# Transfers of the first batches in one queue, weights centred early, and another place for the queries' turn, in a cross-attention kernel in fp32

## The chip, the core and the metric

One core of a Trainium2 chip runs the kernel. The metric is the device time in microseconds of one execution, here the median of three runs. The core has five engines that run side by side, each in the order of its own instructions: TensorE (PE) for matmuls, with results in PSUM; VectorE (DVE); ScalarE (ACT); GpSimd (POOL); and SyncE (SP), which here only issues transfers. Everything is fp32.

## What is computed

For each of 64 batches there are 256 text rows x of width 512 and 256 context rows c of width 384. The reference, cut to what matters (scale is 1/sqrt(512)):

```python
text_p  = einsum('bld,dh->blh', H_l, W_text) + b_text
audio_p = einsum('bsd,dh->bsh', H_a, W_audio) + b_audio
Q = layer_norm(text_p, g1, beta1)
K = layer_norm(audio_p, g2, beta2)
V = audio_p
alpha = softmax(einsum('blh,bsh->bls', Q, K) * scale)
H_hyper = einsum('bls,bsh->blh', alpha, V)
H_hyper = einsum('blh,hk->blk', H_hyper, W_out) + b_out
return layer_norm(H_hyper + H_l, g_out, beta_out)
```

## The kernel before

**Projections.** Queries and keys are projected (`ps_q`, `ps_k`), their bias is added, and each row is normalised. The first two batches use `Projection`: whole products, with mean and variance from VectorE's statistics (`moments`, line 234). From the third on `Blocks` (line 409) is used: W_text, W_audio and their biases have had the mean of each of their rows taken away ("centred"), so that a projected row has mean zero and only its squares are summed (`square`, on ScalarE). `Blocks` computes the 2 x 2 block product with seven instead of eight block products; their left sides come from sums over the turned input (`sum_x`, `sum_c`), their right sides from sums over the weights (`weight_sums`), all on GpSimd. `products` writes one PSUM bank of the pool `p_pj` (four banks) for up to two block products; `leave(n)` (line 431) adds block product n into the rows on VectorE, and when both block products of a bank have left, the bank is free for a later `products`.

**Turning.** A matmul contracts over the partitions, so the normalised rows have to be turned. They are stored to DRAM (`store`: `qd`, `kd`), fetched back by four transfers with the rows in squares of 32 (`fetch`: `qq`, `kq`), turned by VectorE in 32 x 32 squares (`turn`: `qT`, `kT`, lines 91 and 394), and ScalarE applies gamma and beta (`affine`, line 401). The inputs of a later batch are loaded in squares (`load_squares`, eight transfers) and turned the same way (`turn_x`, `turn_c`); the exponentials too (`store_e`, `fetch_e`, `turn_e`). Batch 0 is turned by TensorE instead (`turn_rows`).

**Folding.** W_audio and W_out are multiplied once (`turn_weights`, `fold_multiply`, three parts), so that the context `ps_z` = c^T e needs one product more, `ps_y`, for the output. The bias of it is `bao` (`bias_parts`, `fold_bias`).

**Order.** Nothing is planned by a program: the order is that of the text, and each engine keeps it. A prologue treats batches 0 and 1 and the weights. Then the loop runs over b = 0 to 61. In iteration b TensorE does the scores of b, the block products of the queries of b+2, the context of b-1, the block products of the keys of b+2, and the two output products of b-1. Queries and keys of b+1 were normalised and stored an iteration before; here they are fetched, turned and given gamma and beta. The last two batches have their own code, where TensorE turns the exponentials (`transpose_e`).

**Queues.** Nearly all transfers are issued by SyncE, in order, and a transfer that waits for its data holds all behind it. The five bias and gain rows (`ba`, `bt`, `bo`, `go`, `beo`: `row`, broadcast to 128 partitions, 256 KB each) and the five `vectors` are issued by ScalarE among its own work. Eight semaphores serve all transfers in turn, in the order of the program: a transfer is issued only when the one eight places before it has landed, whichever engine issues it.

**PSUM.** Eight banks: `p_pj` four, `p_at` two (scores, context, turns by TensorE), `p_y` two (output, fold).

Of the kernel before, what the change touches and what calls it, by code (L numbers as in the profile page):

```python
# [15 lines left out]
P = 128  # L16
SQ = 32
# [5 lines left out]
def kernel(  # L23
# [72 lines left out]
    def load_squares(b):  # L96
        xq = blk.tile([P, L // SQ, D // NQ], F32, tag="xq", name=f"xq_{b}")
        cq = blk.tile([P, S // SQ, DA // NQ], F32, tag="cq", name=f"cq_{b}")
        squares(xq, x[b])
        squares(cq, c[b])  # L100
        return xq, cq
# [23 lines left out]
    def row(v, name):  # L125
        t = const.tile([P, H], F32, tag=name, name=name)
        nc.scalar.dma_start(t, v.rearrange("(o h) -> o h", o=1).broadcast_to([P, H]))
        return t
# [7 lines left out]
    nc.sync.dma_start(c_0, c[0].rearrange("(t p) d -> p t d", p=P))  # L136
    wa_sb = weight_by_square(w_audio, AC, "wa", nc.sync)
    ba_sb = row(b_audio, "ba")
    nc.sync.dma_start(x_0, x[0].rearrange("(t p) d -> p t d", p=P))
    wt_sb = weight_by_square(w_text, DC, "wt", nc.sync)  # L140
    blocks = {1: load_squares(1)}
    wo_sb = weight_by_square(w_out, HC, "wo", nc.sync)

    columns = const.tile([P, 5, HC], F32, tag="columns", name="columns")

    def load_columns():
        for n, v in enumerate((g1, beta1, g2, beta2, b_audio)):
# [19 lines left out]
    def turn_rows(rows_sb, chunks, name, copy):  # L167

        ar = work.tile([P, 2, chunks, P], F32, tag="y" if chunks == DC else "kT", name=f"{name}r")
        T = work.tile([P, chunks, 2 * P], F32, tag=name, name=f"{name}_0")  # L170
        for t in range(2):
            arrange(ar[:, t], rows_sb[:, t, :], chunks, copy)
        for lo in range(0, chunks, 2):
            n = min(2, chunks - lo)
            ps = p_at.tile([P, 2, 2 * P], F32, tag="at", name="ps_rows")
            for j in range(n):
                for t in range(2):
                    nc.tensor.transpose(ps[:, j, bass.ts(t, P)], ar[:, t, lo + j, :], ident)
            nc.scalar.copy(T[:, lo : lo + n, :], ps[:, :n, :])
        return T  # L180

# [44 lines left out]
    def fold_bias(part):  # L226

        ps = p_y.tile([P, D], F32, tag="y", name="ps_bao")
# [73 lines left out]
    class Projection:  # L302


        def __init__(self, name, b, srcT, w_sb, bias, nch, nt):
# [3 lines left out]
            self.centred = b > 1  # L309
# [144 lines left out]
    class Attention:  # L454
# [4 lines left out]
        def scores(self):  # L459
            self.sc = p_at.tile([P, LT, S], F32, tag="at", name="ps_sc")  # L460
# [43 lines left out]
        def transpose_e(self):  # L504
            self.ps_e = p_at.tile([P, ST, L], F32, tag="at", name="ps_e")
# [79 lines left out]
    def text(b, xT):  # L585
        return Projection("q", b, xT, wt_sb, bt_sb, DC, LT)

    def audio(b, cT):
        return Projection("k", b, cT, wa_sb, ba_sb, AC, ST)

# [269 lines left out]
```

## Time and profile before

| what | us |
|---|---|
| median of 3 runs (lowest, highest) | 1468.34 (1467.51, 1476.27) |
| the profiled execution: time, span | 1472.76, 1471.0 |
| first matmul | 8.58 |
| first scores | 53.33 |
| second scores | 72.85 |
| third scores | 100.64 |
| scores of the last iteration's successor (batch 62) | 1427.40 |
| last scores (batch 63) | 1443.66 |
| mean granted TensorE clock | 0.995 |

The profile is one execution. Each matmul in fp32 appears as several records (x16 for eight score products). "Releaser" is what ended an engine's idle time. PEld is the load of the stationary operand, which goes on beside matmuls.

### The profile page before, as it was taken

To read this page: it belongs to the slowest core of one execution; us is meant where nothing else is said; L and a number is where in the kernel's file an instruction comes from. 1 tells how busy PE (TensorE), PEld (TensorE's weight loads), DVE (VectorE), ACT (ScalarE), POOL (GpSimd) and SP (SyncE) were. 2 spreads that over 40 slices of the span, in tenths; PEclk is the share of its full clock that TensorE was granted. 3 is DMA by queue.
4 is the path that set the end of the run, shared out by engine and by line. 5 is a ranking of instruction groups with operands and counts; after the bars stand their busy time and mean duration, and the time that the engine had idled before them with its cause. 6 is when DMAs were issued, how large, how long until landed. Compare 5 with 4: busy or idle time off the path is not lost. (4 is left out here: it accounts for less than half of the span.)

```text
span 1471.0 us, 20463 instructions
## 1 busy us (share of the span) xinstructions
PE 1437.6 (98%) x5777; PEld 1097.4 (75%) x5777; DVE 1213.2 (82%) x2077; ACT 697.1 (47%) x1663; POOL 692.6 (47%) x1037
## 2 busy tenths in 40 slices
PE   7999999999999999999999999999999999999996
PEld 3577877877877777877877777777777777877873
DVE  4768888888888788888888797888888888888886
ACT  2435445445455355455455354355455355355352
POOL 1544454454454454454454453554554554454452
PEclk9999999999999999999999999999999999999999
DMA  8587777777787788887887777877877877878872
GB/s 193 151 223 204 225 233 213 230 234 205 242 241 201 236 236 207 240 233 208 237 243 199 238 231 201 242 209 226 245 223 211 246 232 214 239 216 224 241 217 80
DMA packets 450260, 322.41 MB, mean 219 GB/s; under 512 B 154724, under 2 KB 382564, under 8 KB 450148
## 3 DMA queue, kind: packets, MB, share of 16 engines
q1 hardware_dynamic: 449328, 319.79, 76.7%
q10 hardware_dynamic: 820, 1.32, 0.5%
q8 instruction: 47, 0.77, 0.2%
q14 instruction: 65, 0.53, 0.1%
HBM read 204.09 MB, written 116.92 MB: 218 GB/s over the span
## 5 line engine op out<-in xcount | busy, mean ns | idle before, releaser
L297 POOL TENSOR_SCALAR ve<-var 128x2 f32<-128x2 f32 x124 | 26.9, 217 | 680.3 <-ACT junk L335 680.3
L542 PE MATMUL ps_y<-wao,zT 128*128 128x512 f32 x768 | 340.3, 592 | 0.0
L401 ACT ACTIVATE qT<-qT,columns 128x256 f32<-128x256 f32 x256 | 132.9, 589 | 404.7 <-DVE qT L91 404.7
L542 PEld LDWEIGHTS ps_y<-wao,zT 128*128 128x128 f32 x768 | 145.8, 190 | 156.1 <-issue 142.8
L463 PEld LDWEIGHTS ps_sc<-kT,qT 128*128 128x128 f32 x1024 | 195.2, 191 | 55.1 <-issue 22.7
L463 PE MATMUL ps_sc<-kT,qT 128*128 128x256 f32 x1024 | 232.4, 380 | 1.5 <-ACT zT L532 1.5
L438 DVE TENSOR_TENSOR kr<-ps_k,kr 128x512 f32<-128x512 f32 x372 | 185.3, 512 | 24.7 <-DVE kr L438 0.9
L91 DVE STREAM_TRANSPOSE qT<-qq 128x1024 f32<-128x1024 f32 x64 | 79.7, 1245 | 151.0 <-DMA qq<-qd 151.0
L438 DVE TENSOR_TENSOR qr<-ps_q,qr 128x512 f32<-128x512 f32 x372 | 182.4, 504 | 14.7 <-PE ps_q L427 3.8
L525 PE MATMUL ps_z<-eT,c 128*128 128x256 f32 x768 | 176.6, 379 | 0.8 <-ACT eT L514 0.7
L480 ACT ACTIVATE e<-ps_sc,nmx 128x256 f32<-128x256 f32 x128 | 59.5, 469 | 238.0 <-DVE nmx L473 238.0
L427 PE MATMUL ps_q<-wtsum,xsum 128*128 128x256 f32 x744 | 170.7, 379 | 0.0
L427 PE MATMUL ps_k<-wa,cT 128*128 128x256 f32 x620 | 164.6, 380 | 0.0
L604 POOL TENSOR_TENSOR x<-x,bao 128x512 f32<-128x512 f32 x128 | 161.0, 1280 | 3.5 <-DMA x<-in_x_dram 3.5
L525 PEld LDWEIGHTS ps_z<-eT,c 128*128 128x128 f32 x768 | 145.8, 190 | 21.6 <-ACT eT L514 0.9
L427 PEld LDWEIGHTS ps_q<-wtsum,xsum 128*128 128x128 f32 x744 | 141.4, 190 | 19.2
L299 POOL TENSOR_TENSOR rstd<-ve,nhalf 128x2 f32<-128x2 f32 (+1 forms) x193 | 136.6, 708 | 16.0
L401 ACT ACTIVATE kT<-kT,columns 128x256 f32<-128x256 f32 x256 | 132.2, 591 | 3.4 <-DVE kT L91 3.4
L427 PEld LDWEIGHTS ps_k<-wa,cT 128*128 128x128 f32 x620 | 118.2, 191 | 16.2
L427 PE MATMUL ps_q<-wt,xT 128*128 128x256 f32 x496 | 117.2, 379 | 0.0
L363 ACT ACTIVATE kr<-kr,rstd 128x512 f32<-128x512 f32 x124 | 82.8, 715 | 69.9 <-POOL rstd L299 69.9
L427 PE MATMUL ps_k<-wasum,csum 128*128 128x256 f32 x372 | 102.6, 385 | 11.0 <-DVE qr L438 11.0
(113 smaller groups left out, 2228.6 us busy)
## 6 DMA issues: line engine op xcount, KB each, us to landing
x<-in_x_dram SPq DMA_DIRECT2D x64, 512.0 KB, 4.9
kd<-kr SPq DMA_DIRECT2D x64, 512.0 KB, 7.0
kq<-kd SPq DMA_DIRECT2D x256, 128.0 KB, 3.0
qd<-qr SPq DMA_DIRECT2D x64, 512.0 KB, 7.2
qq<-qd SPq DMA_DIRECT2D x256, 128.0 KB, 2.6
xq<-in_x_dram SPq DMA_DIRECT2D x252, 128.0 KB, 2.8
out_dram<-y SPq DMA_DIRECT2D x63, 512.0 KB, 6.0
c<-in_ctx_dram SPq DMA_DIRECT2D x64, 384.0 KB, 5.4
```

The source lines that it names most:

```text
L91: nc.vector.transpose(dst.rearrange("p k (b j) -> p b k j", j=SQ), src.rearrange("p b (k i) -> p b k i", k=chunks),)
L297: nc.gpsimd.tensor_scalar(ve, var, EPS, None, ALU.add)
L299: nc.gpsimd.tensor_tensor(r, ve, nhalf[:, :n], ALU.pow)
L363: nc.scalar.mul(row, row, self.r[t])
L401: nc.scalar.activation(self.T[:, k, :], self.T[:, k, :], AF.Identity, bias=bet[:, k : k + 1], scale=gam[:, k : k + 1],)
L427: nc.tensor.matmul(bank[:, j, :], lhsT=side, rhs=w, start=(i == 0), stop=(i == len(pairs) - 1))
L438: add = lambda o, i0, i1: nc.vector.tensor_tensor(o, i0, i1, ALU.add)
L463: nc.tensor.matmul(self.sc[:, t, :], lhsT=self.qT[:, k, bass.ts(t, P)], rhs=self.kT[:, k, :], start=(k == 0), stop=(k == HC - 1),)
L480: nc.scalar.activation(self.e[:, t, :], self.sc[:, t, :], AF.Exp, bias=self.nmx[:, t : t + 1], accum_out=self.den[:, t : t + 1],)
L525: nc.tensor.matmul(ps[:, j, :], lhsT=self.c_sb[:, s, bass.ts(lo + j, P)], rhs=self.eT[:, s, :], start=(s == 0), stop=(s == ST - 1),)
L542: nc.tensor.matmul(ps, lhsT=self.zT[:, k, bass.ts(t, P)], rhs=wao_sb[:, k, :], start=(k == 0), stop=(k == AC - 1),)
L604: nc.gpsimd.tensor_tensor(xb[:, t, :], xb[:, t, :], bao_sb, ALU.add)
```

## The change

- `row` and the five `vectors` are issued by SyncE. c of batch 0 is loaded in two halves, with W_audio between them. The other transfers of the prologue stand in the order in which their data is wanted; W_out and `bo` go behind the store of the keys of batch 0, and `go`, `beo` to the end of the prologue. `load_squares` takes c before x.
- `RowTurn` takes the place of `turn_rows`: batch 0 is turned row tile by row tile, each followed by its product.
- `means` is done on ScalarE (a sum with scale -1/512), and `centre` adds. W_audio and `ba` are centred, and the weight sums made, before the keys of batch 1; W_text and `bt` before its queries. Batch 1 is then projected by `Blocks`.
- Two parts of the fold stand before the queries of batch 1, the third behind them.
- In the loop the fetches of queries and keys of b+1 are issued behind `store_e` instead of ahead of the scores. `q[b + 1].turn()` stands behind all seven `leave` and `square` of the queries of b+2 (it stood between `leave(5)` and `leave(3)`), and its `affine` behind the context's copies.
- At the end, the last scores and both `transpose_e` take banks of `p_pj`, and `fold_bias` does too.

The diff, cut; the functions `text` and `audio` are gone, and `at`, `done`, `last` are the batches b, b-2 and b-1:

```diff
     def load_squares(b):
         xq = blk.tile([P, L // SQ, D // NQ], F32, tag="xq", name=f"xq_{b}")
         cq = blk.tile([P, S // SQ, DA // NQ], F32, tag="cq", name=f"cq_{b}")
+        squares(cq, c[b])
         squares(xq, x[b])
-        squares(cq, c[b])
         return xq, cq
 ...
-        nc.scalar.dma_start(t, v.rearrange("(o h) -> o h", o=1).broadcast_to([P, H]))
+        nc.sync.dma_start(t, v.rearrange("(o h) -> o h", o=1).broadcast_to([P, H]))
 ...
     c_0 = cin.tile([P, ST, DA], F32, tag="c", name="c_0")
-    nc.sync.dma_start(c_0, c[0].rearrange("(t p) d -> p t d", p=P))
+    c_rows = c[0].rearrange("(t p) d -> p t d", p=P)
+    nc.sync.dma_start(c_0[:, :1], c_rows[:, :1])
     wa_sb = weight_by_square(w_audio, AC, "wa", nc.sync)
+    nc.sync.dma_start(c_0[:, 1:], c_rows[:, 1:])
     ba_sb = row(b_audio, "ba")
     nc.sync.dma_start(x_0, x[0].rearrange("(t p) d -> p t d", p=P))
     wt_sb = weight_by_square(w_text, DC, "wt", nc.sync)
+    bt_sb = row(b_text, "bt")
     blocks = {1: load_squares(1)}
-    wo_sb = weight_by_square(w_out, HC, "wo", nc.sync)
-
     columns = const.tile([P, 5, HC], F32, tag="columns", name="columns")
-
-    def load_columns():
-        for n, v in enumerate((g1, beta1, g2, beta2, b_audio)):
-            nc.scalar.dma_start(
-                vectors[n * HC : (n + 1) * HC].rearrange("k (q i) -> k q i", q=NQ),
-                v.rearrange("(q k i) -> k q i", q=NQ, i=SQ),
-            )
+    for n, v in enumerate((g1, beta1, g2, beta2, b_audio)):
+        nc.sync.dma_start(
+            vectors[n * HC : (n + 1) * HC].rearrange("k (q i) -> k q i", q=NQ),
+            v.rearrange("(q k i) -> k q i", q=NQ, i=SQ),
+        )
 ...
+    class RowTurn:
+
+
+        def __init__(self, rows_sb, chunks, name):
+            self.rows, self.chunks = rows_sb, chunks
+            tag = "y" if chunks == DC else "kT"
+            self.ar = work.tile([P, 2, chunks, P], F32, tag=tag, name=f"{name}r")
+            self.T = work.tile([P, chunks, 2 * P], F32, tag=name, name=f"{name}_0")
+
+        def tile(self, t):
+            ar = self.ar[:, t]
+            arrange(ar, self.rows[:, t, :], self.chunks, nc.vector.tensor_copy)
+            ps = p_at.tile([P, self.chunks, P], F32, tag="at", name="ps_rows")
+            for j in range(self.chunks):
+                nc.tensor.transpose(ps[:, j, :], ar[:, j, :], ident)
+            nc.scalar.copy(self.T[:, :, bass.ts(t, P)], ps)
 ...
-        mv = const.tile([P, n, 2], F32, tag=name, name=name)
+        m = const.tile([P, n], F32, tag=name, name=name)
         for k in range(n):
-            moments(mv, rows[:, k, :], k)
-        return mv
-
-    def centre(rows, mv, n):
+            junk = work.tile([P, H], F32, tag="junk", name="junk")
+            nc.scalar.activation(
+                junk, rows[:, k, :], AF.Identity, scale=-1.0 / H, accum_out=m[:, k : k + 1]
+            )
+        return m
+
+    def centre(rows, m, n):
         for k in range(n):
-            nc.vector.tensor_scalar(rows[:, k, :], rows[:, k, :], mv[:, k, 0:1], None, ALU.subtract)
+            nc.vector.tensor_scalar(rows[:, k, :], rows[:, k, :], m[:, k : k + 1], None, ALU.add)
 ...
-            self.centred = b > 1
+            self.centred = b > 0
 ...
-    cT[0] = turn_rows(c_0, AC, "cT", nc.vector.tensor_copy)
-    bt_sb = row(b_text, "bt")
-    load_columns()
-    k[0] = audio(0, cT.pop(0))
+    c_turn = RowTurn(c_0, AC, "cT")
+    x_turn = RowTurn(x_0, DC, "xT")
+    k[0] = Projection("k", 0, c_turn.T, wa_sb, ba_sb, AC, ST)
+    q[0] = Projection("q", 0, x_turn.T, wt_sb, bt_sb, DC, LT)
+    c_turn.tile(0)
     k[0].multiply(0)
-    xT[0] = turn_rows(x_0, DC, "xT", nc.vector.tensor_copy)
+    c_turn.tile(1)
+    k[0].multiply(1)
+    mean_wa = means(wa_sb, AC, "mwa")
+    k[0].evict(0)
     war = blk.tile([P, AC, HC, P], F32, tag="kq", name="war")
     for a in range(AC):
         arrange(war[:, a], wa_sb[:, a, :], HC, nc.gpsimd.tensor_copy)
-    mean_wa = means(wa_sb, AC, "mwa")
-    k[0].evict(0)
-    k[0].multiply(1)
+    x_turn.tile(0)
+    x_turn.tile(1)
     k[0].evict(1)
     k[0].scales()
-    q[0] = text(0, xT.pop(0))
     q[0].multiply(0)
-    k[0].normalise()
-    k[0].store()
-    cT[1] = turn_c(1)
-    q[0].evict(0)
     q[0].multiply(1)
-    xT[1] = turn_x(1)
-    q[0].evict(1)
-    q[0].scales()
-    k[0].fetch()
-    g1_sb, be1_sb, g2_sb, be2_sb, bac_sb = take_columns()
-
-    for v in (g2_sb, be2_sb):
-        nc.vector.tensor_scalar(v, v, scale, None, ALU.mult)
-    waT = turn_weights()
-    q[0].normalise()
-    q[0].store()
-    mean_wt = means(wt_sb, DC, "mwt")
-    k[1] = audio(1, cT.pop(1))
-    for t in range(ST):
-        k[1].multiply(t)
-        k[1].evict(t)
-    k[1].scales()
-    bo_sb = row(b_out, "bo")
-    k[1].normalise()
-    q[0].fetch()
-    k[1].store()
-    blocks[2] = load_squares(2)
-    k[1].fetch()
-    k[0].turn()
-    k[0].affine(g2_sb, be2_sb)
-    q[1] = text(1, xT.pop(1))
-    q[1].multiply(0)
-    q[1].evict(0)
-    q[1].multiply(1)
-    part = bias_parts()
-    q[1].evict(1)
-    q[1].scales()
-    q[0].turn()
-    centre(wt_sb, mean_wt, DC)
-    fold_multiply(0)
-    fold_multiply(1)
-    fold_evict(0)
-    q[1].normalise()
-    q[1].store()
-    q[1].fetch()
-    q[0].affine(g1_sb, be1_sb)
-    fold_evict(1)
-    fold_multiply(2)
-    fold_evict(2)
-    wt_blocks = weight_sums(wt_sb, DC // 2, "wtsum")
-    xT[2] = turn_x(2)
-    xs = {2: sum_x(xT[2])}
-    for v, name in ((bt_sb, "mbt"), (ba_sb, "mba")):
-        v = v.rearrange("p (o h) -> p o h", o=1)
-        centre(v, means(v, 1, name), 1)
-    blocks[3] = load_squares(3)
-    bao_sb = fold_bias(part)
+    ba_row = ba_sb.rearrange("p (o h) -> p o h", o=1)
+    bt_row = bt_sb.rearrange("p (o h) -> p o h", o=1)
+    mean_ba = means(ba_row, 1, "mba")
     centre(wa_sb, mean_wa, AC)
     wa_blocks = weight_sums(wa_sb, 1, "wasum")
     for n, k2 in ((2, 0), (3, 1), (5, 1), (4, 0)):
         wa_blocks[n].append(wa_sb[:, 2, k2 * H2 : (k2 + 1) * H2])
+    k[0].normalise()
+    k[0].store()
+    wo_sb = weight_by_square(w_out, HC, "wo", nc.sync)
+    bo_sb = row(b_out, "bo")
+    k[0].fetch()
+    blocks[2] = load_squares(2)
+    mean_wt = means(wt_sb, DC, "mwt")
+    mean_bt = means(bt_row, 1, "mbt")
+    centre(ba_row, mean_ba, 1)
+    q[0].evict(0)
+    cT[1] = turn_c(1)
+    cs = {1: sum_c(cT[1])}
+    q[0].evict(1)
+    q[0].scales()
+    centre(wt_sb, mean_wt, DC)
+    centre(bt_row, mean_bt, 1)
+    waT = turn_weights()
+    wt_blocks = weight_sums(wt_sb, DC // 2, "wtsum")
+    q[0].normalise()
+    q[0].store()
+    q[0].fetch()
+    xT[1] = turn_x(1)
+    xs = {1: sum_x(xT[1])}
+    k[1] = Blocks("k", 1, cs.pop(1), wa_blocks, ba_sb)
+    k[1].products(1, 2)
+    k[1].leave(1)
+    k[1].products(6, 5)
+    k[1].leave(6)
+    k[1].leave(2)
+    k[1].leave(5)
+    k[1].products(7, 3)
+    k[1].leave(3)
+    k[1].leave(7)
+    k[1].products(4)
+    g1_sb, be1_sb, g2_sb, be2_sb, bac_sb = take_columns()
+    k[1].leave(4)
+    k[1].square()
+    k[1].scales()
+
+    for v in (g2_sb, be2_sb):
+        nc.vector.tensor_scalar(v, v, scale, None, ALU.mult)
+    k[0].turn()
+    k[1].normalise()
+    k[1].store()
+    k[1].fetch()
+    k[0].affine(g2_sb, be2_sb)
+    blocks[3] = load_squares(3)
+    fold_multiply(0)
+    fold_evict(0)
+    fold_multiply(1)
+    fold_evict(1)
+    part = bias_parts()
+    xT[2] = turn_x(2)
+    xs[2] = sum_x(xT[2])
     cT[2] = turn_c(2)
-    cs = {2: sum_c(cT[2])}
+    cs[2] = sum_c(cT[2])
+    q[0].turn()
+    q[0].affine(g1_sb, be1_sb)
+    q[1] = Blocks("q", 1, xs.pop(1), wt_blocks, bt_sb)
+    q[1].products(1, 2)
+    q[1].leave(1)
+    q[1].products(6, 5)
+    q[1].leave(6)
+    q[1].leave(2)
+    q[1].leave(5)
+    q[1].products(7, 3)
+    q[1].leave(3)
+    q[1].leave(7)
+    q[1].products(4)
+    q[1].leave(4)
+    q[1].square()
+    q[1].scales()
+    fold_multiply(2)
+    fold_evict(2)
+    bao_sb = fold_bias(part)
+    q[1].normalise()
+    q[1].store()
+    q[1].fetch()
     go_sb = row(g_out, "go")
     beo_sb = row(beta_out, "beo")
 ...
         at = Attention(b)
-        if b:
-            q[b + 1].fetch()
-            k[b + 1].fetch()
         at.scores()
 ...
         at.exponentials()
         at.store_e()
+        if b:
+            q[b + 1].fetch()
+            k[b + 1].fetch()
         at.fetch_e()
 ...
         q2.products(7, 3)
-        q[b + 1].turn()
-        q[b + 1].affine(g1_sb, be1_sb)
-        q2.products(4)
         q2.leave(3)
         q2.leave(7)
+        q2.products(4)
         q2.leave(4)
+        q2.square()
+        q[b + 1].turn()
         at.reciprocals()
         if last:
             last.context()
-        q2.square()
+        q[b + 1].affine(g1_sb, be1_sb)
 ...
-        ps = p_y.tile([P, D], F32, tag="y", name="ps_bao")
+        ps = p_pj.tile([P, D], F32, tag="pj", name="ps_bao")
 ...
-            self.ps_e = p_at.tile([P, ST, L], F32, tag="at", name="ps_e")
+            self.ps_e = p_pj.tile([P, ST, L], F32, tag="pj", name="ps_e")
 ...
-    end.scores()
+    end.scores(end=True)
```

More of the change, by code (lines that the diff above doesn't have):

```diff
@@ L165, in arrange @@
         )
[L167 to L180, printed above, removed]
+    class RowTurn:
[11 more added lines that the diff above has]
+            nc.scalar.copy(self.T[:, :, bass.ts(t, P)], ps)
     def turn_weights():
@@ L457, in __init__, with scores @@
             self.xb, self.c_sb = rows[b]
-        def scores(self):
-            self.sc = p_at.tile([P, LT, S], F32, tag="at", name="ps_sc")
+        def scores(self, end=False):
+            if end:
+                self.sc = p_pj.tile([P, LT, S], F32, tag="pj", name="ps_sc")
+            else:
+                self.sc = p_at.tile([P, LT, S], F32, tag="at", name="ps_sc")
             for t in range(LT):
@@ L583, in store @@
             )
[L585 to L589, printed above, removed]
     def turn_x(b):
```

## The prediction

> **What bounds the kernel now.** I read the page first, then TensorE's waits, then TensorE's rows in order of time, then the rows of all engines around its longest wait, then one undisturbed iteration, and last the end of the run. The page's totals say that TensorE is the bound:
>
> ```profile
> span 1471.0 us, 20463 instructions
> PE 1437.6 (98%) x5777; PEld 1097.4 (75%) x5777; DVE 1213.2 (82%) x2077; ACT 697.1 (47%) x1663; POOL 692.6 (47%) x1037
> ```
>
> So only 33.4 us are idle, and a change can take away idle time, time at a lowered clock, or matmul work, and little else. The chain of waits gives the work of one iteration of the loop, at full clock:
>
> ```profile
> 1013.30 6.04 PE ps_q L427 x28
> 1021.94 4.75 PE ps_k L427 x22
> 1026.69 5.15 PE ps_y L542 x12
> 1031.84 3.45 PE ps_sc L463 x16
> ```
>
> The context product lies between the first two (8.64 - 6.04 = 2.60), so an iteration is 21.99, and 1009.85 to 1031.84 in the chain is just that: nothing but matmuls. Of the 62 loop iterations, the first has no context and no output product (14.24), the other 61 have 21.99. TensorE's waits:
>
> ```profile
> PE ps_k L427 <- DVE qr L438: 11.0, 11, 3.1
> PE ps_rows L178 <- DVE cTr L162: 8.6, 1, 8.6
> PE ps_sc L463 <- ACT zT L532: 1.5, 1, 1.5
> PE ps_k L317 <- DMA wa<-in_L_xattn_W_audio_dram: 1.3, 1, 1.3
> PE ps_q L317 <- DMA wt<-in_L_xattn_W_text_dram: 0.9, 1, 0.9
> ```
>
> The first row is the one in the loop. Score products start at 53.33, 72.85 and 100.64 in TensorE's rows, and at 1427.40 behind the loop. So the first iteration took 19.52 (5.28 over its work), the second 27.79 (5.80 over), and the other 60 took 1326.76, 7.4 over 60 x 21.99. The first two, in the rows in order of time:
>
> ```profile
> 52.67 0.35 ACTq L127 DMA_DIRECT2D go<-in_L_xattn_g_out_dram  x1
> 56.48 1.33 SPq L88 DMA_DIRECT2D kq<-kd  x3
> 57.91 0.40 SPq L373 DMA_DIRECT2D qd<-qr  x1
> 61.54 1.78 SPq L88 DMA_DIRECT2D qq<-qd  x4
> 66.03 1.25 DVE L91 STREAM_TRANSPOSE qT<-qq 128x1024 f32<-128x1024 f32 x1 [4.11 <-DMA qq<-qd]
> 67.19 1.64 DVE L438 TENSOR_TENSOR qr<-ps_q,qr 128x256 f32<-128x256 f32 x3
> 68.45 1.19 PE L427 MATMUL ps_k<-wasum,csum 128*128 128x256 f32 x2 [2.88 <-DVE qr L438]
> 72.85 4.42 PE L463 MATMUL ps_sc<-kT,qT 128*128 128x256 f32 x16
> ```
>
> VectorE sits in the turn of the queries (line 91) until their fetch lands; three block sums stand behind it (`leave` 3, 7, 4), and these free the PSUM banks for which the audio products wait. The fetch is late because SyncE stood 9.7 us in a wait for `go`, which ScalarE issued only at 52.67 (SyncE's own waits). After each such wait the granted clock is lower (0.76 and 0.55 in 65 to 75 us, 0.66 in 90 to 95). In a late iteration the same turn waits too, mostly without reaching TensorE:
>
> ```profile
> 1021.75 1.25 DVE L91 STREAM_TRANSPOSE qT<-qq 128x1024 f32<-128x1024 f32 x1 [2.37 <-DMA qq<-qd]
> ```
>
> **The change, part by part.** Times from the span's start.
>
> *The start (c split, `ba` behind it in the same queue).* The first audio product began at 11.62, with 384 KB of c, 768 KB of W_audio and 256 KB of `ba` before or beside it. Now 192 + 768 KB lie ahead. The 448 KB less at the 243 GB/s of 5 to 10 us are 1.85 us; as x is also moved in that time, up to 2.9. I take 2.3: 9.3. Here a rule bears. First the row: c took 7.2 us to land with `ba` on ScalarE's queue beside it, against 5.4 for the same 384 KB in the loop. The Trainium skill (DMA: Bandwidth & Descriptors, Issuing engines are not separate DMA queues) says that transfers of all issuing engines run on the same 16 DMA engines, so a second queue saves only issue time. By the rule alone the move of ten transfers (five rows, five vectors) to SyncE is a loss: ten issues of 0.26 to 0.52 us, some 4 us of SyncE. By the row it gains the order. I take both: the gain here, and the 4 us in SyncE's times below, where the wait for `go` (9.7) is gone in return.
>
> *From there to the first scores.* First product 5.1 at the cold clock (11.62 to 16.66 before), to 14.4; three transposes and a 0.5 us copy, to 15.4; second product 2.6, to 18.0; x's transposes and a copy, 1.1: text products at 19.1 (before 21.17). W_text must be there: 3 MB at 190 to 240 GB/s from 2.5 us are 15.5 to 18.5. Then TensorE: text 6.9, weight turns 2.1, batch 1's audio as block products 4.75 (was 5.15), vectors 0.2, two folds 6.9, text blocks 6.04 (was 6.87), third fold 3.4, bias 0.9: scores at 50.3 instead of 53.3, of which 1.2 is saved work. What must be ready: VectorE ends centring W_audio at about 21.6 (three at 0.77) and the c turn at 25.3; GpSimd's sums (3.3 and 2.1 from the same groups' rows) end at 27.4, TensorE needs them at 29. W_text's centring (2.67) ends at 30.5, its sums (5.4) and x's (3.3) at 39; TensorE needs the latter at 41. The nine means moved to ScalarE (0.65 each, by the squares' rows) fall where it was idle. If one of these covers is gone, TensorE waits for GpSimd, which I bound at 0 and 3 us and take as 0.
>
> *The second scores.* This is the chain that I think is late next. Queries 0 are normalised at 30.8; their store is behind batch 2's loads, 34.4. Stores took 4.0 here before, 7.2 in the median: 5.5, to 40. Fetch to landing 4.5, turn 1.25: 45.8. VectorE's block sums for queries 1 stand behind this turn, 3.9: 49.7; squares 1.3, scales 1.2, normalise 1.4: 53.6; store 6.3: 60; fetch 4.5: 64.5; query turn 1.25 and key turn 1.3 on VectorE, query affine 2.1 and the first key piece 0.5 on ScalarE: scores at 68.4. TensorE has finished at 50.3 + 14.24 = 64.5, and waits 3.9. The clock rule: TensorE: Matmul & The Clock Gate (Part 1) says that the clock falls after an idle window of some 3.4 us; in this trace idles of 2.88 and 3.11 were enough, followed by 6.0 and 3.4 us at half clock, which cost 3.0 and 1.7. By the rule a wait of up to 3.4 would be free of this, by the rows not; I charge 2.3. Second scores 68.4 (was 72.85), third at 68.4 + 21.99 + 2.3 = 92.7 (was 100.64): **-7.9** up to there.
>
> *The loop.* The query turn goes behind `leave` 3, 7, 4, so the banks are free before VectorE waits for a fetch; the 11 waits have no cause left. Both fetches are put behind `store_e`, which waits for the exponentials. SyncE before, counted from the scores' start: query fetch 7.8 (held till then by the store's landing), key fetch 9.7, `store_e` 11.7. After: exponentials end at 6.9, so `store_e` 7.0, query fetch 7.8, key fetch 9.6, e's fetch 11.5. The queries land at the same 12.1 as before, when VectorE has just done its sums (11.3): it waits 0.8 instead of 2.4, and the key turn comes about 1 us sooner (14.4 for 15.5). ScalarE: squares 11.4 to 12.8, context copies to 13.8, query affine to 15.9, key affine to 18; scores need them at 22. Loads and stores behind are issued 2 to 3 us sooner, as `store_e` no longer stands behind the fetches. All covers have 3 us or more. **-7.4.**
>
> *The end.* The last scores and e's transposes take banks of the other pool. Before:
>
> ```profile
> 1443.05 0.83 ACT L532 COPY zT<-ps_z 128x512 f32<-128x512 f32 x2
> 1443.66 3.72 PE L463 MATMUL ps_sc<-kT,qT 128*128 128x256 f32 x16 [1.50 <-ACT zT L532]
> ```
>
> The keys' affine runs 1441.07 to 1443.15 in four pieces, so the scores can follow it at once, and VectorE's closing work hangs on them: **-1.5.**
>
> Sum: -16.8. The profiled execution took 1472.76 (span 1471.0), so 1456.0 for one like it. It is 4.4 above the median of 1468.34; straight from the median it would be 1451.5. The 7.4 us of the loop differ from run to run, and a faster run has fewer of them to lose, so the truth lies between: **1453**. About 1% (14.7 us, below 1453.7 or above 1483) is what a measurement here can tell from no change.
>
> **The rivals.**
> 1. *The sum holds* (0.62): 1448 to 1457, by the store's landing (4.0 or 7.2, twice) and the cold clock.
> 2. *The loop's waits stay* (0.13). VectorE has 19.0 us of work in each 22; if its lateness comes from elsewhere, the reordering moves it. Against: in each shown wait it sits at the query turn. -7.9 - 1.5: 1459.
> 3. *The head gives nothing* (0.16): GpSimd's sums are late for the block products, or queries 1 stay behind batch 3's loads in the single queue, and the second scores stay near 72.9. What remains is the second iteration's wait and clock, 4, and 7.4 + 1.5: 1455 to 1459.
> 4. *Slower* (0.09): the fetches behind `store_e` come too late in every iteration. Place: the query and key turns on VectorE. It has 3.0 us to spare per iteration; every us that it waits beyond that is lost 60 times. If the turns wait 3.8 us, 0.8 x 60 = 48 are lost and 17 gained: 1484. That is decided where the query fetch lands about 15 us after the scores' start instead of 12; for it speaks only that everything is now in one queue behind ScalarE.
>
> **How the numbers follow.** Case 1 lies between 1448 and 1457 with its middle at 1452.5 to 1453, nearer to 1451.5 if the loop's waits in the median run were those of the profile: I put 0.44 of its 0.62 below the line, and 0.06 of case 3, where the second scores come a little sooner: faster 0.50. The rest of 1 and 3 and all of 2: same 0.41. Slower 0.09. The range leaves out case 4 and the ends: 1447 to 1460.
>
> **What would show it.** Text products at about 19 us and first scores near 50; second scores at 66 to 70 with the idle time named after the keys' affine or the query fetch; no row in which TensorE's audio products wait for the text sums on VectorE; the waits for the query fetch on VectorE down from 151 us in total to about 50; iterations of 21.99 throughout; no wait of the last scores for the context copy. Wrong: iterations above 22.2 in the mean, or a wait of TensorE for GpSimd's sums in the head.

## The result, and the profile after

The changed kernel takes 1451.24 us (median of 4 runs, 1449.66 to 1451.91), the kernel before 1470.21 beside it (4 runs, 1467.51 to 1476.27): ratio 0.9864, 95% interval 0.983 to 0.9898. The profiled execution took 1451.83 (span 1450.0, before 1471.0). The totals of its page:

```profile
span 1450.0 us, 20424 instructions
PE 1429.6 (99%) x5799; PEld 1098.4 (76%) x5799; DVE 1223.8 (84%) x2061; ACT 731.0 (50%) x1689; POOL 699.0 (48%) x1041
```

TensorE is idle for 20.4 us instead of 33.4, and busy for 8.0 less. Its waits (what it waited for: us in total, times, longest):

```profile
PE ps_rows L180 <- DVE cTr L161: 4.0, 1, 4.0
PE ps_k L321 <- DMA wa<-in_L_xattn_W_audio_dram: 2.9, 1, 2.9
PE ps_q L431 <- POOL xsum L276: 0.9, 2, 0.7
...
PE ps_q L431 <- DVE xT L91: 0.7, 1, 0.7
...
PE ps_sc L470 <- ACT kT L405: 0.6, 1, 0.6
```

No audio product waits for VectorE's text sums, and no score for the context copy. The stretch from 120 to 1400 us, by engine (busy time and instructions, then granted clock, DMA share and GB/s), of the kernel before:

```profile
120.00:1400.00 1280.00, 1275.00 (x5214) 989.21 (x5213) 1080.45 (x1849) 622.99 (x1497) 620.33 (x924) 1.00 0.79 226
```

and of the changed kernel:

```profile
120.00:1400.00 1280.00, 1280.00 (x5244) 996.10 (x5243) 1110.03 (x1868) 655.72 (x1517) 627.70 (x933) 1.00 0.81 227
```

TensorE has not one idle moment there. Its rows in the chain of waits are those of before, 21.98 apart (114.77 to 136.75):

```profile
114.77 6.04 PE ps_q L431 x28
123.40 4.75 PE ps_k L431 x22
...
133.30 3.45 PE ps_sc L470 x16
136.75 6.04 PE ps_q L431 x28
```

Where the 21.0 us of span come from is read from the starts of the score products in TensorE's rows (us). "Loop over" is what the 59 iterations from the fourth to the 63rd scores took beyond 59 x 21.985; the same columns serve for the experiments.

| kernel | 1st | 2nd | 3rd | 4th | loop over | 63rd to last | span |
|---|---|---|---|---|---|---|---|
| before | 53.33 | 72.85 | 100.64 | 122.62 | 7.7 | 16.26 | 1470.98 |
| after | 48.81 | 63.13 | 87.28 | 111.15 | 0.0 | 14.60 | 1450.00 |
| e1 only the turn moved | 52.46 | 68.86 | 92.31 | 115.51 | 17.5 | 17.23 | 1476.33 |
| e2 only the fetches moved | 52.94 | 71.09 | 101.00 | 122.99 | 5.2 | 17.59 | 1470.23 |
| e3 changed, turn put back | 48.92 | 64.59 | 92.86 | 114.85 | 6.4 | 15.63 | 1461.40 |
| e6 before, rows on SyncE | 50.97 | 65.22 | 94.53 | 116.52 | 8.3 | 15.29 | 1464.56 |
| e4 changed, rows on ScalarE | 53.45 | 71.53 | 96.19 | 118.17 | 0.0 | 14.60 | 1457.03 |
| e5 changed, end's banks put back | 49.89 | 64.57 | 90.13 | 114.01 | 0.1 | 15.28 | 1453.77 |
| e7 changed, batch 1 whole | 49.37 | 63.70 | 87.13 | 110.10 | 0.0 | 14.60 | 1448.95 |
| e8 changed, loads behind stores | 49.23 | 63.55 | 88.66 | 112.54 | 0.0 | 14.60 | 1451.39 |
| e9 changed, squares of batch 4 later | 48.73 | 63.06 | 86.50 | 108.49 | 0.0 | 14.60 | 1447.34 |
| e11 changed, run again | 49.41 | 63.73 | 87.16 | 110.47 | 0.6 | 14.60 | 1449.95 |
| e12 e7 again | 49.53 | 63.85 | 87.30 | 109.28 | 0.0 | 14.60 | 1448.13 |
| e10 e7 and e9 | 50.60 | 64.93 | 88.37 | 110.35 | 0.0 | 14.61 | 1449.20 |

After against before: first scores -4.5, second -9.7, third -13.4, fourth -11.5, 63rd -19.1, last -20.8. So the head gave 11.5 net, having given 1.9 of 13.4 back in the third iteration; the loop gave 7.7 and the end 1.7. After, e3, e5, e8, e9 and e11 have the same code up to the first scores, and these lie between 48.73 and 49.89: a difference of 1 us in that column is no finding.

The second iteration, from the second to the third scores, sorts the kernels by the turn's place alone: with the old place (before, e2, e3, e6) it takes 27.8 to 29.9 us, with the new one (all others) 23.4 to 25.6, whatever the queue and the fetches. So some 4 us of the head's gain are the turn's (28.27 in e3, 24.15 after).

The head after the change, rows of all engines in order of time (start, us, engine, line, operation):

```profile
48.81 3.62 PE L470 MATMUL ps_sc<-kT,qT 128*128 128x256 f32 x16
...
51.89 0.38 SPq L377 DMA_DIRECT2D qd<-qr  x1
...
54.65 1.79 SPq L88 DMA_DIRECT2D qq<-qd  x4
...
59.24 1.24 DVE L91 STREAM_TRANSPOSE qT<-qq 128x1024 f32<-128x1024 f32 x1
...
63.13 3.90 PE L470 MATMUL ps_sc<-kT,qT 128*128 128x256 f32 x16
```

Queries 1 are stored at 51.89, fetched from 54.65 (the fetch is issued only when the store has landed, so that took at most 2.8), and turned at 59.24 without a wait. The eight loads ahead of the store had been issued by 50.45, and the 16 DMA engines are busy only 0.23 of the time from 52 to 53 us: those loads were nearly through. One iteration later the same chain is late:

```profile
65.14 2.85 SPq L88 DMA_DIRECT2D cq<-in_ctx_dram  x4
68.02 1.93 SPq L88 DMA_DIRECT2D xq<-in_x_dram  x4
70.00 0.45 SPq L106 DMA_DIRECT2D x<-in_x_dram  x1
70.49 0.47 SPq L107 DMA_DIRECT2D c<-in_ctx_dram  x1
71.07 0.40 SPq L377 DMA_DIRECT2D qd<-qr  x1
...
78.49 1.80 SPq L88 DMA_DIRECT2D qq<-qd  x4
...
83.11 1.25 DVE L91 STREAM_TRANSPOSE qT<-qq 128x1024 f32<-128x1024 f32 x1 [8.02 <-DMA qq<-qd]
```

Ten loads stand ahead of the store of queries 2 in the one queue, the last issued 0.1 us before it. ScalarE had normalised them at 65.78; the store is issued at 71.07, lands 7.4 later behind those loads, and VectorE waits 8.02 us. The second and third iterations take 24.15 and 23.87 us instead of 21.99; the experiment e9 shows how much of that is this wait.

### The profile page after: what moved, and what is told of

Its sections match the earlier page's. It is cut to its first block, busy times and chain, and to the rows that moved or that the text cites. A ratio compares the mean times of both kernels' runs of the same rounds, so it can differ in the third digit from the quotient of the medians.

```text
span 1450.0 us, 20424 instructions
## 1 busy us (share of the span) xinstructions
PE 1429.6 (99%) x5799; PEld 1098.4 (76%) x5799; DVE 1223.8 (84%) x2061; ACT 731.0 (50%) x1689; POOL 699.0 (48%) x1041
## 4 chain that ended last, share of the span: by engine, by line
PE 92%; DMA 4%; DVE 1%; SPq 1%; issue 1%; POOL 0%; ACT 0%; POOLq 0%; DVEq 0%
PE ps_q L431 25%; PE ps_y L549 22%; PE ps_k L431 20%; PE ps_sc L470 15%; PE ps_z L532 11%; DMA qd<-qr 1%; DMA cq<-in_ctx_dram 1%; SPq L88 1%; DMA wt<-in_L_xattn_W_text_dram 1%; DMA ed<-e 0%; DMA wo<-in_L_xattn_W_out_dram 0%; DVE kr L442 0%; DVE qr L442 0%; DMA kq<-kd 0%; DVE y L577 0%
## 5 line engine op out<-in xcount | busy, mean ns | idle before, releaser
L442 DVE TENSOR_TENSOR qr<-ps_q,qr 128x512 f32<-128x512 f32 x378 | 188.2, 512 | 48.6 <-PE ps_q L431 36.6
L339 ACT ACTIVATE junk<-qr 128x512 f32<-128x512 f32 x126 | 79.4, 630 | 271.5 <-DVE qr L442 271.5
L442 DVE TENSOR_TENSOR kr<-ps_k,kr 128x512 f32<-128x512 f32 x378 | 188.3, 512 | 27.2 <-PE ps_k L431 4.9
L431 PE MATMUL ps_q<-wtsum,xsum 128*128 128x256 f32 x756 | 173.7, 379 | 0.9 <-POOL xsum L276 0.9
L605 POOL TENSOR_TENSOR x<-x,bao 128x512 f32<-128x512 f32 x128 | 171.7, 1362 | 4.0 <-DMA x<-in_x_dram 4.0
L303 POOL TENSOR_TENSOR rstd<-ve,nhalf 128x2 f32<-128x2 f32 (+1 forms) x193 | 141.8, 734 | 16.0
L405 ACT ACTIVATE qT<-qT,columns 128x256 f32<-128x256 f32 x256 | 132.9, 591 | 11.6 <-DVE qT L91 11.5
L577 DVE SCALAR_TENSOR_TENSOR y<-y,rstd,beo 128x512 f32<-128x512 f32 x128 | 103.6, 810 | 4.9 <-POOL rstd L303 4.6
```

The source lines that it names most:

```text
L303: nc.gpsimd.tensor_tensor(r, ve, nhalf[:, :n], ALU.pow)
L339: nc.scalar.activation(junk, self.rows[:, t, :], AF.Square, scale=1.0 / math.sqrt(H), accum_out=self.var[:, t : t + 1],)
L405: nc.scalar.activation(self.T[:, k, :], self.T[:, k, :], AF.Identity, bias=bet[:, k : k + 1], scale=gam[:, k : k + 1],)
L431: nc.tensor.matmul(bank[:, j, :], lhsT=side, rhs=w, start=(i == 0), stop=(i == len(pairs) - 1))
L442: add = lambda o, i0, i1: nc.vector.tensor_tensor(o, i0, i1, ALU.add)
L577: nc.vector.scalar_tensor_tensor(self.y[:, t, :], self.y[:, t, :], self.r[t], beo_sb, ALU.mult, ALU.add)
```

## Experiments on the loop: the turn, the fetches, or both

My theory had the turn's place ("behind the text sums") as the cause of the loop's gain, with the fetches behind `store_e` as an extra without much weight. The rivals were that the fetches do it, or that it needs both.

**e1**: before, with the turn alone moved. **e2**: before, with the fetches alone moved. **e3**: the changed kernel with the turn put back (and `square` behind the context).

```diff
e1 (from the kernel before)          e2 (from the kernel before)
         q2.products(7, 3)                    at = Attention(b)
-        q[b + 1].turn()             -        if b:
-        q[b + 1].affine(...)        -            q[b + 1].fetch()
-        q2.products(4)              -            k[b + 1].fetch()
         q2.leave(3)                          at.scores()
         q2.leave(7)                 ...
+        q2.products(4)                       at.store_e()
         q2.leave(4)                 +        if b:
+        q2.square()                 +            q[b + 1].fetch()
+        q[b + 1].turn()             +            k[b + 1].fetch()
         at.reciprocals()                     at.fetch_e()
 ...
-        q2.square()
+        q[b + 1].affine(...)
```

> The kernel before, with the loop's new place for the queries' turn alone (behind leave 3, 7, 4 and square; affine behind the context's copies); the fetches stay ahead of the scores, the prologue and the end stay. If the turn's place freed the loop: from the third scores on every iteration takes 21.99, about 7.5 us less over these 60, and the two waits of 2.9 and 3.1 us in the first two iterations shrink too, so 9 to 13 us less than before. If it was the fetches' place behind store_e: less than 3 us.

> The kernel before, with the fetches of queries and keys moved behind store_e and nothing else. If the turn's place did it: VectorE still sits in the turn with three block sums behind it, waits of TensorE for them remain, within 3 us of before. If the fetches' place did it: the loop's 7.4 us go, and the time falls by 6 to 8.

> The changed kernel with the turn (and affine, context copies, square) back in its old place. If the turn's place is needed: waits of TensorE's audio products for the text sums return, 3 to 8 us over the loop, and the second iteration, whose query fetch lands late, grows by 3 or more. If the fetches' place suffices: no such row, within 2 us of the changed kernel.

On one chip, in one series of runs, beside 1478.08 for the kernel before: e1 1479.72, ratio 1.0018 (1.0 to 1.0035); e2 1474.14, 0.9983 (0.9967 to 0.9998); e3 1463.43, 0.9904 (0.9873 to 0.9934). By "loop over" the two moves make a square: neither 7.7 (before) or 8.3 (e6, with the loop of before, in the series of e1 to e3), turn alone 17.5, fetches alone 5.2 (and 6.4 with the new head, e3), both 0.0. These are single profiled executions, and the kernel before was 5 us slower in this series than in its own profile, so the 9 to 10 us that the turn alone loses are not exact. But e1 is no faster than before in 20 runs, although its fourth scores come 7.1 sooner: its loop is no better. (The changed kernel, run again as e11, had 0.6 in place of 0.0.) TensorE's waits in e1 say in part where:

```profile
PE ps_q L427 <- POOL xsum L272: 2.3, 11, 0.7
...
PE ps_q L427 <- DVE xT L91: 1.7, 4, 0.6
```

The rows of audio products waiting for `qr` are gone, as I had said; text products wait for x's turn and sums instead. Dividing e1's 59 iterations at the first matmul of each product and taking off the work of an undisturbed one (3.45, 6.04, 2.60, 4.75), the excess lies 2.8 in the scores, 8.0 in the text product, 4.4 in the context product and 2.0 in the audio product; in the kernel before, all of it (7.6) lies in the audio product. The two rows name only 4.0 of the 17.5 us; most of the rest are stalls inside groups of matmuls, for which the profile gives no releaser. That they follow the query turn is seen by counting: of e1's iterations in that stretch, the 15 behind a turn that began less than 15 us after its scores lose at most 0.01 us, the 7 behind one of 17 us or more lose 0.64 to 1.72 each. So VectorE is late as before, and the lateness comes out a few instructions further on. What makes it late is to be seen in one late round of e1, in the rows of all engines:

```profile
1221.01 1.25 DVE L91 STREAM_TRANSPOSE qT<-qq 128x1024 f32<-128x1024 f32 x1 [0.59 <-DMA qq<-qd]
...
1228.74 2.02 SPq L88 DMA_DIRECT2D cq<-in_ctx_dram  x4
...
1232.37 0.42 SPq L373 DMA_DIRECT2D qd<-qr  x1
...
1240.98 1.80 SPq L88 DMA_DIRECT2D qq<-qd  x4
...
1245.41 1.25 DVE L91 STREAM_TRANSPOSE qT<-qq 128x1024 f32<-128x1024 f32 x1 [3.26 <-DMA qq<-qd]
```

From one turn to the next this takes 24.4 us, one of the three longest of e1's loop (22.3 in the mean). The steps follow one another: query turn, affines, normalising of the next queries (done at about 1229 on ScalarE), their store, its landing, the fetch, the next turn. Two steps are SyncE's. It issues the store some 3.4 us after the normalising, as it is still at the loads; and it issues the fetch only when the store has landed, 8.6 later, and everything written behind the fetch, `store_e` and the loads first, waits with it. SyncE's waits of the kernel before and of e1 show the same two large rows; before:

```profile
SPq L88 <- DMA qd<-qr: 312.3, 63, 6.7
SPq L88 <- DMA ed<-e: 165.4, 62, 3.1
```

After the change they are nearly gone:

```profile
SPq L501 <- ACT e L487: 307.3, 60, 5.4
...
SPq L88 <- DMA qd<-qr: 12.5, 3, 5.2
...
SPq L88 <- DMA ed<-e: 4.9, 1, 4.9
```

SyncE now waits for ScalarE's exponentials, that is, it is early. The fetches' place alone does this, in e2:

```profile
SPq L494 <- ACT e L480: 258.0, 60, 5.2
...
SPq L88 <- DMA qd<-qr: 9.6, 3, 5.0
```

The whole loop says the same. From the start of the scores to the first query fetch of the iteration, SyncE's rows of iterations 4 to 61 have 7.5 us in the mean before (6.1 to 9.4), 11.3 in e1 (9.4 to 13.2), 7.4 in e2 (6.1 to 7.8) 7.5 in e3 (6.7 to 7.9) and 6.1 after; to `store_e` 11.4, 15.3, 6.9, 7.0 and 5.6. With the fetches at their old place a late store delays `store_e` and the loads, and these delay the next store: the lateness is handed on (in part: in e1 a turn of 17 us or more is followed by one of 16.8 in the mean, one below 15 by one of 15.0). With the fetches behind `store_e` the store lands while SyncE would be waiting for the exponentials anyhow. But that alone leaves the audio products behind a turn that waits, in e2:

```profile
1084.89 1.25 DVE L91 STREAM_TRANSPOSE qT<-qq 128x1024 f32<-128x1024 f32 x1 [2.77 <-DMA qq<-qd]
...
1087.32 0.67 PE L427 MATMUL ps_k<-wasum,csum 128*128 128x256 f32 x2 [0.22 <-DVE qr L438]
```

For the loop both moves are needed: by these rows one ends the cycle, the other takes the sums out from behind what is left of the wait. The move of the turn also moves `affine`, `square` and one `products`; no run takes these apart. VectorE's wait for the query fetch is 151.0 us in all before, 116.5 in e1, 157.7 in e2 and 24.9 after.

## Experiments on the head and the end

**e6**: the kernel before with the five rows and five vectors on SyncE's queue. **e4**: the reverse, the changed kernel with them on ScalarE's.

```diff
e6, in row and load_columns:         e4, in row and for vectors:
-        nc.scalar.dma_start(        -        nc.sync.dma_start(
+        nc.sync.dma_start(          +        nc.scalar.dma_start(
```

> The kernel before with the five rows and the five vectors issued by SyncE at the same places of the text. If the wait for go delayed batch 1: SyncE's wait for go of 9.7 us is gone, the keys of batch 1 are fetched near 47 instead of 56.5 and the queries near 54 instead of 61.5; the first two iterations lose most of their 5.3 and 5.8 us over their work, 6 to 10 us in all. If something else held the queries back: the third scores stay within 2 us of 100.6.

> The changed kernel with the five rows and five vectors issued by ScalarE again, at the same places of the text. If the one queue carries the first iterations: the start is later by 1 us or more, and some transfer waits again for one that ScalarE issues late, so the third scores come 3 to 8 us later and the time is 4 to 9 us above the changed kernel's. If the order of the text now suffices: within 1.5 us of it.

e4 took 1458.45, ratio 0.9798 (0.9771 to 0.9825) beside 1489.06 for the kernel before (on the chip of e1 to e3, in a later series of runs); e6, one time, 1466.34 beside 1478.08. In spans, e4 gives back 7.0 of the 21.0 us (e7, in e4's series, took 1450.85: 7.6 in times), and e6 gains 6.4 without any other part of the change. The start of e4, TensorE's rows:

```profile
6.48 0.87 PE L180 MATMUL ps_rows<-ident,cTr 128*128 128x128 f32 x3 [6.48 <-DVE cTr L161]
11.07 4.92 PE L321 MATMUL ps_k<-wa,cT 128*128 128x512 f32 x6 [3.72 <-DMA wa<-in_L_xattn_W_audio_dram]
```

With c in two parts but the rows on ScalarE, the first audio product begins at 11.07 (11.62 before, 7.82 after). With the rows on SyncE and c whole (e6), at 8.27. So at the first product the gain is the queue, and the halves of c (with the turning by row tile) add half a microsecond. At the text products this half microsecond is gone again:

```profile
8.27 4.35 PE L317 MATMUL ps_k<-wa,cT 128*128 128x512 f32 x6 [1.67 <-DMA wa<-in_L_xattn_W_audio_dram]
...
16.87 5.39 PE L317 MATMUL ps_q<-wt,xT 128*128 128x512 f32 x12 [0.23 <-DMA wt<-in_L_xattn_W_text_dram]
```

This is e6; the changed kernel's text products begin at 17.98, 1.1 later. Later in e4, around 50 to 72 us:

```profile
53.48 6.26 SPq L88 DMA_DIRECT2D xq<-in_x_dram  x4
...
55.37 0.37 ACTq L127 DMA_DIRECT2D go<-in_L_xattn_g_out_dram  x1
...
60.34 0.38 SPq L377 DMA_DIRECT2D qd<-qr  x1
...
71.53 6.29 PE L470 MATMUL ps_sc<-kT,qT 128*128 128x256 f32 x16 [3.67 <-ACT kT L405]
```

ScalarE reaches the load of `go` late, SyncE waits 4.5 us for it (and 7.5 for `bo`), so that four x loads take 6.26 us (1.93 after the change); the store of queries 1 leaves 8.5 us later than in the changed kernel (the first scores only 4.6 later), and TensorE waits 3.67, with a granted clock of 0.66 from 70 to 80 us. That is the wait which I had taken from the kernel before, and e6 shows it gone with the queue alone: its second scores come at 65.22, at full work distance from the first (14.25). Its second iteration, which I had expected to gain too, took 29.31 (27.79 before): with the turn at its old place the queue does not help there. Why SyncE's fetches and loads wait for `go` at all, whose data they do not need and which stands behind them in the text, is put down here to the shared semaphores; the waits are shown, this reason is not tested.

**e5**: the last scores and e's transposes back in the banks of before (`p_pj` to `p_at` in two lines).

> The changed kernel with the last scores and the turns of the exponentials in the two banks of before. If the bank was the wait at the end: TensorE's last scores wait 1.5 us for the context's copy again and the interval from the last scores but one (14.6 us) is 1.5 us longer; everything ahead stays. If the keys' affine was: no difference.

One time, 1455.62. The last scores:

```profile
1426.53 3.72 PE L470 MATMUL ps_sc<-kT,qT 128*128 128x256 f32 x16 [0.52 <-ACT zT L539]
```

The wait comes back with 0.52, and the interval with 0.68 of the 1.66. The other 1.0 isn't the banks': the same end code as before has 16.26 before, 15.29 in e6, 17.23 in e1 and 17.59 in e2, with a wait for the context's copy of 1.5, 0.5, 2.5 and 2.8. What sets this copy's time stays open. Of the 3.8 us that this span lies over that of the changed kernel, 2.9 are there by the fourth scores, where the code is the same.

**e7**: batch 1 projected whole again, as before, instead of by block products, the rest of the change kept. **e12** is e7 again.

```diff
-    k[1] = Blocks("k", 1, cs.pop(1), wa_blocks, ba_sb)
-    k[1].products(1, 2)
 ...
+    k[1] = Projection("k", 1, cT.pop(1), wa_sb, ba_sb, AC, ST)
+    k[1].multiply(0)
+    k[1].evict(0)
+    k[1].multiply(1)
 ... the same for q[1]
```

> The changed kernel with batch 1 projected by whole products (with the centred weights, squares on ScalarE), so without its block products and the sums for them. By the matmul work alone: first scores 1.2 us later (50.0 for 48.8). If GpSimd's sums and VectorE's seven steps were in the way of the second batch: first scores as early or earlier, and the second scores without loss.

> Batch 1 by whole products again, now timed beside the changed kernel. If the block products of batch 1 are worth their matmul work: 1.2 us slower than the changed kernel. If they give it back in the second and third iterations, as the look at this kernel suggests (23.43 and 22.97 us for 24.15 and 23.87): equal or up to 1.5 us faster.

e7, one time: 1450.85. e12, on another chip beside **e11**, the changed kernel again: 1450.37 and 1450.57. The block products of batch 1 give nothing that can be measured: what TensorE saves (1.2 us by my sum) is no larger than the scatter of the head, and in e7 the third iteration takes 22.97 instead of 23.87 (the changed kernel itself takes 23.31 in e11).

> The changed kernel once more, as the measure for the three others on the same chip: 1450 to 1456.

**e8**: in the first iteration the loads go behind both stores, to let the store of queries 2 out sooner.

```diff
         at.fetch_e()
-        if b + 4 < B:
-            blocks[b + 4] = load_squares(b + 4)
-        rows[b + 1] = load_rows(b + 1)
+        if b:
+            load_next(b)
 ...
         k2.store()
+        if not b:
+            load_next(b)
```

> The changed kernel; in the first iteration alone the ten loads for later batches are issued behind the two stores of batch 2 instead of ahead of them. If what the changed kernel still loses in its second and third iterations (24.15 and 23.87 us for 21.99) comes from batch 2's query store, which stood behind these loads from 65.8 to 71.1: VectorE's wait of 8.0 us for the query fetch falls to about 5, the third scores come at about 85.5 instead of 87.3 and the fourth at about 108 instead of 111.2, 3 us less in all (about 1448). If the waits come from GpSimd's sums, which follow the keys' squares: less than 1 us.

It took 1453.31, ratio 0.9768 (0.9743 to 0.9793) beside 1489.06. Against my expectation nothing was gained:

```profile
66.22 0.38 SPq L377 DMA_DIRECT2D qd<-qr  x1
...
76.33 2.84 SPq L88 DMA_DIRECT2D qq<-qd  x4
...
84.42 1.25 DVE L91 STREAM_TRANSPOSE qT<-qq 128x1024 f32<-128x1024 f32 x1 [8.90 <-DMA qq<-qd]
```

The store is issued 4.9 us sooner, but now the ten loads stand between it and the fetch; the turn is at 84.42 instead of 83.11. What is moved has to be put somewhere else than on the same chain.

**e9**: eight of those ten loads (the squares of batch 4) go one iteration later. **e10** is e9 with e7.

```diff
-        if b + 4 < B:
-            blocks[b + 4] = load_squares(b + 4)
+        for n in ((), (4, 5))[b] if b < 2 else (b + 4,):
+            if n < B:
+                blocks[n] = load_squares(n)
```

> The changed kernel; the squares of batch 4 are loaded in the second iteration behind all fetches (with those of batch 5) instead of in the first. If the query fetch of the second iteration is late because these eight loads stand ahead of batch 2's stores and fetches in the queue and in transfer: VectorE's wait of 8 us falls to 4 or less, the second iteration comes down from 24.15 to about 22.7, and 1.5 to 3 us are gained. If the lateness moves on to the next iteration's stores: no gain, or a third or fourth iteration above 22.5.

> Both edits, batch 1 by whole products and the squares of batch 4 an iteration later. If they remove different waits: 2 to 4 us below the changed kernel; if the same: no better than the better of the two.

Beside 1464.19 for the kernel before: e9 1449.45, ratio 0.9902 (0.9885 to 0.9918); e11 1450.57, 0.9909 (0.9895 to 0.9924); e10 1450.36, 0.9907 (0.9892 to 0.9921). In e9 the same rows read:

```profile
65.73 0.37 SPq L377 DMA_DIRECT2D qd<-qr  x1
...
71.24 1.97 SPq L88 DMA_DIRECT2D qq<-qd  x4
...
76.14 1.25 DVE L91 STREAM_TRANSPOSE qT<-qq 128x1024 f32<-128x1024 f32 x1 [1.11 <-DMA qq<-qd]
```

VectorE's 8.02 is 1.11, and the third iteration is back at 21.99. Set in the order of this wait, the kernels with both moves and the queue (single executions, us):

| | e9 | e10 | e12 | e7 | e11 | after | e8 | e5 |
|---|---|---|---|---|---|---|---|---|
| VectorE's wait for queries 2 | 1.11 | 2.07 | 4.01 | 6.28 | 6.66 | 8.02 | 8.90 | 9.09 |
| second iteration | 23.44 | 23.44 | 23.45 | 23.43 | 23.43 | 24.15 | 25.11 | 25.56 |
| third iteration | 21.99 | 21.98 | 21.98 | 22.97 | 23.31 | 23.87 | 23.88 | 23.88 |

A wait of up to 4.0 costs nothing, one of 6 to 7 some 1.0 to 1.3 in the third iteration, one of 8 or more 1.9 there and 0.7 to 2.1 in the second. The changed kernel itself stands in two of the columns (after, e11). The 1.45 over in the second iteration stays whatever the wait is. TensorE's wait for x's sums on GpSimd (0.74) is still in it; among the kernels with the new head only e4, whose second scores come 8 us later, is without it. e9's runs (1449.05 to 1450.07) lie below all of e11's (1450.21 to 1451.78), by 1.1 in the median: of my 1.5 to 3 the trace shows the removal, the time somewhat less. The two ratios' intervals overlap, so this is a small gain. e9's median is the lowest of its series; e10 adds nothing to it.

## Why the prediction was right, and where it was not

**The sum.** 16.8 us were forecast and the span lost 21.0; 1453 was 1.8 over the median. That it came out near is partly luck: the second scores came 5.3 us sooner than the sum had them, and the two iterations behind them took 4.0 longer.

**The start: right in kind, small in size, and its cause was half wrong.** I took 2.3 us for c's halves and `ba`'s place together (192 and 256 KB, so 1.0 and 1.3), and put text products at 19.1, first scores at 50.3. It was 3.8, and they came at 17.98 and 48.81. The queue alone gave 3.35 (11.62 to 8.27, e6), the halves with the new turning 0.55 (e4), and at the text products e6 is ahead. Nor does the profile show the cold clock that I gave the first product: the granted clock is 1.00 from 11.62 to 16.66, though that product took 5.04 us and the next of its form 2.66. In weighing the rule that a second issuing queue saves only issue time I charged SyncE 4 us for ten more issues. Whatever these cost, it is outweighed: e6 gains 6.4 and e4 loses 7.0. The larger term is that the loads issued by ScalarE come late behind ScalarE's work while SyncE waits for them (9.7 us for `go` before).

**The second scores: this step failed.** It put stores at 5.5 and 6.3 us, hence queries 1 fetched at 60, the turn at 64.5, a wait of 3.9 and 2.3 for the cold clock. The store took at most 2.8, the fetch was issued at 54.65 and the turn came at 59.24; there was no wait, and the granted clock was 1.00 in each stretch from 50 to 120 us. Forecast 68.4, measured 63.13. The median landing of a store (7.2 before) is that of the loop, where loads are still in transfer ahead of it; here they were nearly through. The clock rule was therefore not put to the test in the changed kernel; e4's 3.67 wait with the clock at 0.66 behind it agrees with either form.

**The third and fourth: not foreseen.** I held all covers of the second iteration to be 3 us or more and let it run at 21.99. It took 24.15, the next 23.87, 4.0 over together. I had counted for queries 0 the loads of batch 2 ahead of their store, and did not count for queries 2 the ten loads ahead of theirs. e9 and the table beside it show that this is what cost the third iteration its 1.9, and the second 0.7 of its 2.16. The rest holds TensorE's wait for GpSimd's sums (0.72), which I had bound at 0 to 3 us, taken as 0, and named as a sign of being wrong.

**The loop: the number right, the reason wrong.** -7.4 forecast, -7.7 measured, and VectorE's wait for the query fetch fell further than forecast (24.9 us in 34 waits, 8.0 of them in the second iteration, where I had 0.8 in each and about 50 in all). But the sentence that the 11 waits "have no cause left" once the turn is behind the sums is refuted by e1, in whose loop TensorE loses 17.5 us. I had named the sums behind the waiting instruction, but not asked what made the wait: the round over SyncE, in which a late store makes the next one late. The fetches behind `store_e`, which I treated as harmless and as the place of the slower rival, are what ends that. The rival's price, 60 times any wait beyond VectorE's spare 3 us, did not arise: the turn began 10.9 us after the scores in the mean of iterations 4 to 61, where the sum had the landing at 12.1, and SyncE had time over. That price was also summed wrongly: 48 lost and 17 gained from the median of 1468.34 are 1499, not 1484.

**The rivals.** That the loop's losses stay is what happens with either of its two moves alone (e1, e2), not with both. That the head gives nothing, for GpSimd's sums or queries stuck behind loads, has its second half in the second iteration, one batch later than I had put it.

**The end**: -1.5 forecast, -1.7 measured; the banks are 0.7 of it by e5, and the rest is within what this stretch differs from run to run, so the hit is luck in size. **No gain from saved work** in batch 1's block products, for which the sum had 1.2 (e7, e12).

## What to carry to other kernels

When an instruction waits for a landing, look not only at what is queued behind it but follow the data round: if its own result feeds, through an in-order issuing engine, the next such wait, then lateness is handed on, and moving the wait to a quieter place only moves where it shows. Put into each issuing queue nothing that must wait for a landing ahead of something that is ready, and give no late engine a load for which the main queue has to stand still. And for a store that a later step needs soon, count what is ahead of it in the same queue at that place, rather than take a median.

## What the hardware showed that I had not expected

- The landing of one 512 KB store took at most 2.8 us with the loads ahead nearly through (51.89 to 54.65) and 7.4 behind ten loads (71.07 to 78.49); in e9, with two loads ahead, at most 5.5 (its fetch followed `store_e`, not the landing).
- The kernel before took 1464.19, 1470.21, 1478.08 and 1489.06 us in four series of runs (1478.08 and 1489.06 on the same chip), with runs spread over 1.7 us in the steadiest and 15 in the widest. The changed kernel and those that keep both loop moves and the queue lie between 1449.45 and 1455.62 in three of them. The changed kernel's own gain was 1.4% in one series and 0.9% in another. That a loop which hangs on landings feels the chip and one that TensorE fills doesn't is my reading of it; the kernel before was not profiled in the slower series, so this stays open.
- A change can take away the one wait that the profile had named in the loop and gain nothing: in e1 no row of audio products on text sums is left, its loop is 9 to 10 us longer, and its time is 1.0018 of the kernel before.
